# A four-layer graph network on one core: in the third layer, a copy and a read moved by one turn, and a row stored in two parts

## The chip, the core and the metric

The kernel runs on one core of a Trainium2 chip. A core has five engines that run their own instruction streams and wait for each other by semaphores: TensorE (PE, its weight loads PEld), VectorE (DVE), ScalarE (ACT), GpSimd (POOL) and SyncE (SP, which here only issues DMAs). GpSimd issues the gathers (indirect DMAs), SyncE all other transfers. The metric is the device time of one execution in microseconds.

## What is computed

The reference takes 6250 nodes with 256 features and 100000 edges and applies four graph layers; after each, the layer's output is added to its input and normalised. The third layer, which the change is in, is two graph attention passes, one after the other:

```python
def _gat_layer(h_in, W, a_s, a_d, b, src, dst, n):
    h = (h_in @ W).reshape(n, Hh, Cc)                 # 4 heads of 64
    alpha_s = jnp.sum(h * a_s, axis=-1)
    alpha_d = jnp.sum(h * a_d, axis=-1)
    e = leaky_relu(alpha_s[src] + alpha_d[dst], 0.2)  # a self loop for each node is in src, dst
    ex = jnp.exp(e - segment_max(e, dst)[dst])
    alpha = ex / segment_sum(ex, dst)[dst]
    return segment_sum(h[src] * alpha[:, :, None], dst).reshape(n, Hh * Cc) + b
h = gelu(_gat_layer(x, W0, ...)); h = gelu(_gat_layer(h, W1, ...))
x = _layernorm(x + h)
```

The fourth layer needs, for each target, the sum of `x` over its edges. The kernel gets part of that as a dense product with a matrix of edge counts, and it makes this matrix beside the third layer.

## The kernel before

Nodes are cut into 50 blocks of 125 targets. Each block's edges, sorted by target, are 16 chunks of 128 edges; the few that don't fit are shared by 25 blocks. A pass of the third layer handles a block in four pieces of four chunks, so 200 pieces a pass. Each piece goes through steps in a fixed distance:

- `piece2` gathers its edges' rows of the table `hs` (features, source score, target score) by four indirect DMAs on GpSimd into one of ten buffers `g` (L929).
- `steps_of` adds the target's score to the source's (`e`, L2152), applies the leaky slope (`r`, L2154), takes exponentials on ScalarE (L2156, L2157), and multiplies the rows by them (L2160, VectorE).
- `one_hots` (L938, VectorE) makes the matrix that sends each edge to its target, and TensorE adds the rows up by target into a bank `ps` (L2227; L2220 adds the self loop). There are two such banks, so the block after next needs a bank back.
- `finish2` reads the finished sums (L2044 to L2046), and for each pair of blocks adds the bias, applies Gelu and multiplies by the next weights (first pass), or normalises and prepares the tables of the fourth layer (second pass).

`keys2` gets the targets' scores to the edges, a block ahead. SyncE loads the block's keys into `kb` (two buffers); ScalarE turns them into masks, in two halves of two pairs of instructions (`node_hots`, L947 and L948); TensorE multiplies them with the scores in 48 small products into a bank `pe`, 24 for each half (L2185); ScalarE copies the bank to `ends_d` (L2190, three buffers). There is one bank `pe`: the products of the next block can't begin before this copy.

`count_edges` makes the count matrix, a step now and then beside the pieces. VectorE makes weighted one-hots (L1995), TensorE adds them up (L2005). Three ranges of 500 targets share a float32 word (one byte each), and a row block of 125 sources has two such words. For each word ScalarE copies the sum to an integer (L1981) and spreads its bytes out (L1982) into half of `a_row`, 3000 bytes a source with one buffer. After the second word the whole row block is stored to `a_table`. Every transfer of 125 rows through `move` (L807 to L811) is two DMAs, of 112 and 13 rows.

The order of TensorE's, VectorE's and ScalarE's work is written out by the class `Turns`. A piece, a block's keys or a finish is a generator that names, at each `yield`, the group of work that it goes on with. In each turn the groups are stepped in the order "e", "msg", "fin", "fa", "act", "pe", "ps", "late", "new", "keys". A plain name means the next turn; a number before it ("2act") means so many turns later; a "+" means in this turn, if the group's place has not passed. A turn takes one new piece in, so a block is four turns. `run_pass` adds a block's keys eight turns ahead of its first piece. Turns only set the order on each engine: an engine that is ready runs on into later turns, and another can be turns behind.

So the copy L2190 of a block stands in the second turn after its last small product, and the finish reads a block's sums in the third turn after its last sum.

Of the kernel before, what the change touches and what calls it, by code (L numbers as in the profile page):

```python
# [9 lines left out]
U8 = mybir.dt.uint8  # L10
# [646 lines left out]
def gnn_stack_kernel(ctx: ExitStack, tc: tile.TileContext, ins, out):  # L657
# [13 lines left out]
    nc = tc.nc  # L671
# [4 lines left out]
    B = max(p for p in range(1, P + 1) if N % p == 0)  # L676
# [36 lines left out]
    ND, RB, WORD = 24, 4, 3  # L713
    RW, NR = RB * B, ND // RB
# [28 lines left out]
    with ExitStack() as fast:  # L743
# [885 lines left out]
        with tc.tile_pool(name="f0", bufs=1) as pool, tc.tile_pool(name="f0w", bufs=2) as work, tc.tile_pool(  # L1629
            name="f0v", bufs=1  # L1630
# [316 lines left out]
        def count_edges():  # L1947


            column = ap.tile([P, RW], F16, name="a_column", bufs=1)  # L1950
            nc.vector.scalar_tensor_tensor(
                column.rearrange("p (b n) -> p b n", n=B), iota[:, :RB, None].to_broadcast([P, RB, B]), float(B),
                iota_p[:, None, :B].to_broadcast([P, RB, B]), op0=ALU.mult, op1=ALU.add,
            )
            end, over = (
                ap.tile([P, 3, RW], BF16, name="a_hot", bufs=4).rearrange("p i j -> p (i j)").bitcast(F32)[:, : NB * DC]
                .rearrange("p (b c) -> p b c", c=DC) for _ in range(2)
            )
            nc.vector.tensor_copy(end, idx_s[:, :, :DC])
            unit = [ap.tile([P, NB, DC], F32, name=f"a_unit{w}", bufs=1) for w in range(NW)]  # L1960
            nc.vector.memset(unit[0], 1.0)
            for w in range(1, NW):
                nc.vector.memset(unit[w], 0.0)
            less = ap.tile([P, NB, DC], F32, name="a_less", bufs=1)
            nc.vector.tensor_copy(less, end)
            for r in range(1, NR + 1):
                nc.vector.tensor_single_scalar(over, end, float(r * RW), op=ALU.is_ge)
                nc.vector.scalar_tensor_tensor(less, over, -float(RW), less, op0=ALU.mult, op1=ALU.add)
                for w, by in ((r // WORD, 256.0 ** (r % WORD)), ((r - 1) // WORD, -(256.0 ** ((r - 1) % WORD)))):
                    if w < NW:  # L1970
                        nc.vector.scalar_tensor_tensor(unit[w], over, by, unit[w], op0=ALU.mult, op1=ALU.add)
            yield
            steps = [(s, *slot) for s in range(NB) for slot in slots]
            sts, rows, accs, hots, done = {}, {}, {}, {}, []
            for k in range(len(steps) + 4):
                if done and done[0][2] <= k:
                    s, w, _ = done.pop(0)
                    if w == 0:
                        rows[s] = ap.tile([B, ND * B], U8, name="a_row", bufs=1)
                    word = ap.tile([B, RW], I32, name="a_word", bufs=1)  # L1980
                    nc.scalar.copy(word, accs.pop((s, w))[:B])  # L1981
                    nc.scalar.activation(  # L1982
                        rows[s][:, w * WORD * RW : (w + 1) * WORD * RW].rearrange("p (q j) -> p q j", q=WORD),
                        word.bitcast(U8).rearrange("p (j q) -> p q j", q=4)[:, :WORD, :], AF.Copy,
                        accum_out=counted[:B, s * NW + w : s * NW + w + 1],
                    )
                    if w == NW - 1:
                        move(nc.sync, a_table[s * B : (s + 1) * B, :], rows.pop(s))
                if k < len(steps):
                    s, w, c0, n, _, _ = steps[k]  # L1990
                    if s not in sts:
                        sts[s] = one_hots(ap, key_s[:, s, :DC], DC, DC, 2, BF16, "a_st")
                    hots[k] = ap.tile([P, 3, RW], BF16, name="a_hot", bufs=4)
                    for i in reversed(range(n)):
                        nc.vector.tensor_scalar(  # L1995
                            hots[k][:, i, :], column, less[:, s, c0 + i : c0 + i + 1],
                            unit[w][:, s, c0 + i : c0 + i + 1], op0=ALU.is_equal, op1=ALU.mult,
                        )
                if 0 <= k - 1 < len(steps):
                    s, w, c0, n, first, last = steps[k - 1]  # L2000
                    hot = hots.pop(k - 1)
                    if first:
                        accs[s, w] = apsum.tile([P, 512], F32, name="a_acc", bufs=2)[:, :RW]
                    for i in range(n):
                        nc.tensor.matmul(  # L2005
                            accs[s, w], sts[s][:, c0 + i, :], hot[:, i, :], start=(first and i == 0),
                            stop=(last and i == n - 1),
                        )
                    if last:
                        done.append((s, w, k + 2))  # L2010
                        if w == NW - 1:
                            del sts[s]
                yield
# [15 lines left out]
        for layer in range(2):  # L2029
# [142 lines left out]
            def keys2(b):  # L2172
                kb = work.tile([B, CAP], BF16, name="kb")
                move(nc.sync, kb, keys_d[b : b + 1, :].to_broadcast([B, CAP]))
                yield "2keys"
                ts = kb.rearrange("p (c e) -> p c e", e=P)
                for half in range(2):
                    node_hots(kb, 2 * half)
                    node_hots(kb, 2 * half + 1)
                    yield "pe"  # L2180
                    if half == 0:
                        pe = psum.tile([P, CM, H2], F32, name="pe")
                    for c in range(CM // 2 * half, CM // 2 * (half + 1)):
                        for k in range(3):
                            nc.tensor.matmul(  # L2185
                                pe[:, c, :], ts[:, c, :], ad_parts[:, b, k, :], start=(k == 0), stop=(k == 2)
                            )
                    yield "2act" if half else "+keys"
                ends_d[b] = work.tile([P, CM, H2], F32, name="ends_d", bufs=3)
                nc.scalar.copy(ends_d[b], pe)  # L2190

            def piece2(b, c0, n):
                if c0 == 0:
                    if b % GB == 0:
                        turns.add(shared2(b // GB))
                    held[b] = work.tile([B, 1, D + 8], F32, name="own", bufs=4)
                    move(nc.sync, held[b][:, 0, :], block_rows(table, b))
                g = gp.tile([P, 4, D + 8], F32, name="g")
                for i in reversed(range(n)):
                    gather(g[:, i, :], table[:, :], idx_d[:, b, c0 + i : c0 + i + 1])  # L2200
                yield "2e"
                steps = steps_of(g, n, ends_d[b][:, c0 : c0 + n, :], (c0 // 4) % 2)
                next(steps)
                if c0 == 0:
                    own = held[b]
                    mine = steps_of(own, 1, own[:, :, D + 4 :], 3, B)
                    next(mine)
                yield "msg"
                for _ in steps:
                    pass  # L2210
                if c0 == 0:
                    for _ in mine:
                        pass
                st = one_hots(work, key_d[:, b, c0 : c0 + n], n, 4, ST_BUFS)
                if c0 + n == CM:
                    st_s = one_hots(work, key_d[:, b, CM:], SH, SH, 3, name="st_s")
                yield "ps"
                if c0 == 0:
                    sums[b] = psum.tile([P, 512], F32, name="ps", bufs=2)
                    nc.tensor.matmul(  # L2220
                        sums[b][:B, : D + H2], ident[:B, :B], held[b][:, 0, : D + H2], start=True, stop=False
                    )
                from_all = [(c0 + i, st[:, i, :], g, i) for i in range(n)]
                if c0 + n == CM:
                    from_all = [(-1, st_s[:, h, :], shared[b // GB], h) for h in range(SH)] + from_all
                for c, hot, m, i in from_all:
                    nc.tensor.matmul(  # L2227
                        sums[b][:B, : D + H2], hot, m[:, i, : D + H2], start=False, stop=(c == CM - 1)
                    )
                if c0 + n == CM:  # L2230
                    del held[b], ends_d[b]
                    yield "3fin"
                    yield from finish2(b, layer)

            made = pieces((4, 4, 4, 4))
# [247 lines left out]
```

## Time and profile before

| | us |
|---|---|
| median of 3 runs (lowest, highest) | 5936.43 (5924.23, 5954.35) |
| the profiled execution | 5892.39 |
| its span | 5890.5 |
| start of the third layer's first pass, 2695 to 2775 | 80 |
| its steady part, 2775 to 3895 | 1120 |
| end and start of the second pass, 3895 to 4000 | 105 |
| its steady part, 4000 to 5127 | 1127 |
| end of the third layer, 5127 to 5180 | 53 |
| fourth layer, 5180 to 5890 | 710 |

Over the span TensorE is busy 70%, VectorE 62%, ScalarE 50% and GpSimd 61%, and the mean granted clock of TensorE is 0.836 of full speed. The profiled execution is 44 us faster than the median of the other runs, so a sum made on its rows is carried to the median as a ratio.

In the lines of the profile, a group of instructions has its source line, engine, operation, output and inputs, then "| busy us, mean ns of one | idle us of the engine before them" and what ended that idle time. In lists of waits, "A <- B: us, times, longest" says that A was idle until B. "issue" is idle time that nothing in the profile ended, and "remote" is a release whose source isn't known. A releaser is inferred from the semaphores; where it had long been done, it was another.

### The profile page before, as it was taken

The numbers are of one execution on the slowest core, as the hardware profiler recorded it, in microseconds if no ns is written. First come the engines' busy times: TensorE is split into PE (matmuls) and PEld (weight loads), VectorE is DVE, ScalarE is ACT, GpSimd is POOL, SyncE is SP. The second block draws the span as 40 slices with busy tenths as digits, with TensorE's granted clock in tenths as the row PEclk, the third lists the DMA queues.
The fourth block names the chain that finished last, engine by engine and source line by source line (L and its number), as shares of the span: only waits on it lengthen the run. The fifth ranks groups of instructions, "written<-read, shape, count | busy, mean of one in ns | idle before, by whom it ended". The sixth has DMA issues, their size and how long they took to land. (4 is left out here: it accounts for less than half of the span.)

```text
span 5890.5 us, 79635 instructions
## 1 busy us (share of the span) xinstructions
PE 4107.0 (70%) x25027; PEld 3010.6 (51%) x25027; DVE 3632.0 (62%) x9526; ACT 2948.2 (50%) x7453; POOL 3595.0 (61%) x3710
## 2 busy tenths in 40 slices
PE   0567788875777777773666766656776677769996
PEld 0355666663555566552554554544555555535554
DVE  7786666653767777773656656645766667613454
ACT  4015676882666676662454445533555555422331
POOL 5776666654666666653666666646666666556663
PEclk9788899997888888886777788777878878889998
DMA  6555565554666777763444444434545455477883
GB/s 157 141 165 159 157 158 155 153 149 143 204 204 206 208 211 210 207 189 86 132 135 134 135 137 136 133 101 123 146 139 140 138 147 140 118 197 221 235 238 102
DMA packets 409642, 940.75 MB, mean 160 GB/s; under 512 B 96973, under 2 KB 214331, under 8 KB 409211
## 3 DMA queue, kind: packets, MB, share of 16 engines
q0 software_dynamic: 221184, 670.83, 41.3%
q1 hardware_dynamic: 188026, 264.74, 15.3%
q8 instruction: 201, 3.29, 0.2%
q14 instruction: 231, 1.88, 0.1%
HBM read 848.02 MB, written 87.21 MB: 159 GB/s over the span
## 5 line engine op out<-in xcount | busy, mean ns | idle before, releaser
L929 POOL DMA_INDIRECT g<-hs_table_f,idx_d x1600 | 1527.6, 955 | 920.5 <-issue 453.1
L929 POOL DMA_INDIRECT g<-h_table_f,idx_d x800 | 802.0, 1002 | 435.2 <-issue 212.3
L2227 PE MATMUL ps<-g,st 128*125 128x260 f32 x3200 | 955.0, 445 | 116.6 <-issue 108.9
L929 POOL DMA_INDIRECT g<-kv_table_f,idx_s x784 | 744.8, 950 | 448.8 <-issue 289.4
L2160 DVE TENSOR_TENSOR g<-g,iota_p 128x1024 f32<-128x1024 f32 x400 | 488.4, 1221 | 654.6 <-ACT iota_p L2156 312.4
L2227 PEld LDWEIGHTS ps<-g,st 128*125 128x125 f32 x3200 | 712.7, 224 | 320.9 <-issue 151.0
L2185 PE MATMUL pe<-ad_parts,kb 125*128 125x4 bf16 x4800 | 220.1, 165 | 631.7 <-issue 543.1
L963 PE MATMUL ps<-g,st 128*128 128x256 bf16 (+1 forms) x3648 | 525.2, 300 | 136.3 <-issue 61.3
L929 POOL DMA_INDIRECT g<-x_table_f,idx_d x416 | 397.8, 956 | 289.3 <-issue 158.8
L963 PEld LDWEIGHTS <-st 128*128 128x128 bf16 x4104 | 427.8, 106 | 283.1 <-issue 130.3
L2185 PEld LDWEIGHTS <-kb 125*128 125x128 bf16 x4800 | 185.0, 99 | 721.8 <-issue 603.4
L1920 PE MATMUL ps<-g,st 128*125 128x264 f32 x1600 | 470.2, 442 | 28.1 <-issue 20.2
L947 ACT ACTIVATE kb<-kb,minus 125x512 bf16<-125x512 bf16 x600 | 426.2, 711 | 58.3 <-DMA g<-kv_table_f,idx 20.4
L948 ACT ACTIVATE kb<-kb,ones 125x512 bf16<-125x512 bf16 x600 | 432.6, 721 | 20.6 <-ACT kb L947 1.5
L2393 PE MATMUL d<-cnt,xs 125*128 125x500 bf16 x1800 | 403.7, 378 | 36.5 <-issue 20.4
L938 DVE TENSOR_TENSOR st<-iota_p,key_d 128x500 f32<-128x500 f32 (+1 forms) x550 | 410.6, 747 | 0.0
L1920 PEld LDWEIGHTS ps<-g,st 128*125 128x125 f32 x1600 | 344.9, 220 | 112.3 <-issue 28.9
L1903 DVE TENSOR_TENSOR prod<-g,qe 128x1024 f32<-128x1024 f32 x200 | 243.2, 1216 | 246.5 <-PE ps L1920 96.7
L2156 ACT ACTIVATE iota_p<-r 128x16 f32<-128x16 f32 (+2 forms) x504 | 90.9, 180 | 591.0 <-DVE e L2152 217.6
L1889 PE MATMUL qe<-q,kb 125*128 125x256 bf16 x2400 | 324.0, 288 | 65.6 <-issue 32.5
L1515 ACT ACTIVATE ob<-t_f,s_f 125x128 bf16<-125x128 f16 x800 | 310.3, 388 | 96.1 <-remote 65.1
L1889 PEld LDWEIGHTS <-kb 125*128 125x128 bf16 x2400 | 247.8, 103 | 141.6 <-issue 77.6
(458 smaller groups left out, 8051.4 us busy)
## 6 DMA issues: line engine op xcount, KB each, us to landing
kb<-keys_d_f SPq DMA_DIRECT2D x100, 448.0 KB
g<-hs_table_f,idx_d POOLq DMA_INDIRECT x1600
xs<-x_table_f SPq DMA_DIRECT2D x75, 336.0 KB
kb<-keys_s_f SPq DMA_DIRECT2D x50, 448.0 KB
a_table_f<-a_row SPq DMA_DIRECT2D x50, 328.1 KB
few<-a_table_f SPq DMA_DIRECT2D x75, 218.8 KB
g<-h_table_f,idx_d POOLq DMA_INDIRECT x800
g<-kv_table_f,idx_s POOLq DMA_INDIRECT x784
```

What stands on the lines that cost most here:

```text
L929: nc.gpsimd.indirect_dma_start(out=g, out_offset=None, in_=table, in_offset=bass.IndirectOffsetOnAxis(ap=idx, axis=0))
L938: nc.vector.tensor_tensor(st, iota_p[:, None, :w].to_broadcast([P, n, w]), key[:, :, None].to_broadcast([P, n, w]), op=ALU.is_equal,)
L947: nc.scalar.activation(part, part, AF.Square, bias=minus[:B])
L948: return nc.scalar.activation(part, part, AF.Relu, bias=ones[:B, 0:1], scale=-1.0)
L963: nc.tensor.matmul(ps[:, :m], st[:, i, :], g[:, i, k * D : k * D + m], start=(c0 + i == 0 and k == 2), stop=(c0 + i == CH - 1 and k == 0),)
L1515: nc.scalar.activation(ob[:, i, :], o1[:, i, :], AF.Copy, scale=val_b[:, at])
L1889: nc.tensor.matmul(qe[:, i, :], ts[:, c0 + i, :], q[:, k * D : (k + 1) * D], start=(k == 0), stop=(k == 2))
L1920: nc.tensor.matmul(sums[b][:B, : D + H1], hot, m[:, i, D - H1 :], start=(c == 0), stop=(c == CM - 1))
L2160: nc.vector.tensor_mul(feats, feats, pp[:, :, :, None].to_broadcast([p, n, H2, C2]))
L2185: nc.tensor.matmul(pe[:, c, :], ts[:, c, :], ad_parts[:, b, k, :], start=(k == 0), stop=(k == 2))
L2227: nc.tensor.matmul(sums[b][:B, : D + H2], hot, m[:, i, : D + H2], start=False, stop=(c == CM - 1))
L2393: nc.tensor.matmul(accs[h][q], xs[:, i, j * D + h * P : j * D + (h + 1) * P], cnt[:, i, q * RW : (q + 1) * RW], start=(s + i == 0 and j == 2),
```

## The change

Three edits, all in the third layer's passes.

1. In `keys2`, the copy of the targets' scores to `ends_d` comes three turns after the block's last small product in place of two.
2. In `piece2`, `finish2` begins four turns after the block's last sum in place of three.
3. In `count_edges`, each word of a row block has a buffer of its own of 1500 bytes a source, of which there are two, and is stored right after it is made; before, both words stood in one buffer of 3000 bytes and were stored together.

```diff
@@ count_edges @@
-            sts, rows, accs, hots, done = {}, {}, {}, {}, []
+            sts, accs, hots, done = {}, {}, {}, []
             for k in range(len(steps) + 4):
                 if done and done[0][2] <= k:
                     s, w, _ = done.pop(0)
-                    if w == 0:
-                        rows[s] = ap.tile([B, ND * B], U8, name="a_row", bufs=1)
+                    row = ap.tile([B, WORD * RW], U8, name="a_row", bufs=NW)
                     word = ap.tile([B, RW], I32, name="a_word", bufs=1)
                     nc.scalar.copy(word, accs.pop((s, w))[:B])
                     nc.scalar.activation(
-                        rows[s][:, w * WORD * RW : (w + 1) * WORD * RW].rearrange("p (q j) -> p q j", q=WORD),
+                        row.rearrange("p (q j) -> p q j", q=WORD),
                         word.bitcast(U8).rearrange("p (j q) -> p q j", q=4)[:, :WORD, :], AF.Copy,
                         accum_out=counted[:B, s * NW + w : s * NW + w + 1],
                     )
-                    if w == NW - 1:
-                        move(nc.sync, a_table[s * B : (s + 1) * B, :], rows.pop(s))
+                    move(nc.sync, a_table[s * B : (s + 1) * B, w * WORD * RW : (w + 1) * WORD * RW], row)
@@ keys2 @@
-                    yield "2act" if half else "+keys"
+                    yield "3act" if half else "+keys"
                 ends_d[b] = work.tile([P, CM, H2], F32, name="ends_d", bufs=3)
                 nc.scalar.copy(ends_d[b], pe)
@@ piece2 @@
                 if c0 + n == CM:
                     del held[b], ends_d[b]
-                    yield "3fin"
+                    yield "4fin"
                     yield from finish2(b, layer)
```

## The prediction

> **What bounds the kernel now.** I read the page's busy shares, the stretches of the span by stage, the waits of each engine inside the two attention passes of the third layer, and the timelines of one block. The change touches only these two passes (2775 to 3895 us, and 4000 to 5127 us), so only their limits matter.
>
> The page says that no engine is full over the span. The last line shown here is the row to remember: the small products `pe` keep TensorE idle for 631.7 us, of which 543.1 us ended with no releaser ("issue").
>
> ```profile
> PE 4107.0 (70%) x25027; PEld 3010.6 (51%) x25027; DVE 3632.0 (62%) x9526; ACT 2948.2 (50%) x7453; POOL 3595.0 (61%) x3710
> L929 POOL DMA_INDIRECT g<-hs_table_f,idx_d x1600 | 1527.6, 955 | 920.5 <-issue 453.1
> L2185 PE MATMUL pe<-ad_parts,kb 125*128 125x4 bf16 x4800 | 220.1, 165 | 631.7 <-issue 543.1
> ```
>
> The stretches (length, then busy time and count of PE, PEld, DVE, ACT, POOL, then the granted clock, the DMA share and GB/s) show the same picture in both passes: 1120 and 1127 us for about 47.5 blocks each, so some 23.6 us a block.
>
> ```profile
> 2775.00:3895.00 1120.00, 759.45 (x4749) 568.18 (x4749) 675.05 (x1624) 541.45 (x1219) 724.63 (x762) 0.79 0.48 133
> 4000.00:5127.00 1127.00, 797.60 (x4866) 583.42 (x4865) 757.81 (x1973) 570.92 (x1316) 730.68 (x763) 0.80 0.50 139
> ```
>
> Next, who waits for whom between 2800 and 3880 us (total us, times, longest), first on TensorE, then on ScalarE:
>
> ```profile
> PE pe L2185 <- issue: 263.5, 242, 2.7
> PE ps L2227 <- issue: 38.2, 41, 2.2
> PE pe L2185 <- ACT kb L947: 8.2, 2, 7.3
> PE pe L2185 <- remote: 4.3, 1, 4.3
> ```
>
> ```profile
> ACT ends_d L2190 <- PE ps L2220: 86.2, 17, 9.3
> ACT ends_d L2190 <- PE ps L2227: 66.9, 15, 10.5
> ACT a_row L1982 <- DMA a_table_f<-a_row: 36.5, 7, 12.8
> ```
>
> TensorE is busy 68% of the first pass, and its idle time is nearly all "issue": 263.5 + 38.2 + 12.8 + 8.2 + 1.3 = 324 us in these 1080 us. Waits for another engine or a DMA come to 19 us there, and to 12 us in 4000 to 5120 us. So TensorE has work that is ready all the time. ScalarE's waits for `pe` are long because TensorE is late, not the other way round.
>
> The timelines of TensorE and of GpSimd around 3310 us show what "issue" is:
>
> ```profile
> 3307.54 0.16 PE L2185 MATMUL pe<-ad_parts,kb 125*128 125x4 bf16 x1 [0.54 <-issue]
> 3309.68 0.17 PE L2185 MATMUL pe<-ad_parts,kb 125*128 125x4 bf16 x1 [1.25 <-issue]
> 3312.54 0.78 PE L2220 MATMUL ps<-own,ident 125*125 125x260 f32 x1 [1.25 <-issue]
> 3314.34 3.10 PE L2227 MATMUL ps<-g,st 128*125 128x260 f32 x8
> ```
>
> ```profile
> 3311.34 0.95 POOL L929 DMA_INDIRECT g<-hs_table_f,idx_d  x1 [0.30 <-issue]
> 3314.33 0.95 POOL L929 DMA_INDIRECT g<-hs_table_f,idx_d  x1 [2.04 <-DVE rdens L2044]
> ```
>
> Once a block, during the second half of `pe`, TensorE gets on at one instruction per 0.7 us for some 8 us. That ends about 1.5 us after GpSimd pauses (here at 3312.29), and GpSimd pauses because all ten gather buffers wait for TensorE's sums. The two take turns: 16 gathers at 1.25 us are 20 us, and pauses of 2 to 2.8 and about 1.2 us make 23.6. GpSimd's waits for anything but "issue" in 2800 to 3880 us are some 190 us. This alternation bounds the passes; vector and scalar engines follow it. Why TensorE slows the trace doesn't say.
>
> **The change, part by part.**
>
> *Copy of the targets' scores a turn later* (L2190, 100 copies of 0.21 us). It removes nothing and adds nothing; it moves each copy behind one more piece's two exponentials (0.17 + 0.20 us) and behind the masks L947/L948 of the next block's first half. ScalarE's waits at this copy (189.5 + 149.1 + 82.6 + 45.1 + 9.9 = 476 us over both passes) shrink, but they are slack: credit 0. Its price is the single `pe` bank: the next block's `pe` can't begin before the copy. I lined up, for all 99 pairs, the end of the exponentials behind which the copy will stand with the start of the next block's `pe`. The slack has a median of 4.1 us; it is negative in 21 cases, with 49 us together. That is an upper estimate, as these times still contain the waits that go away: taking each copy's own wait off leaves 13 negative cases with 31 us, of which 19 us lie at pass starts and ends, where TensorE has other cover or waits for gathers. I take +8 us, ends 0 and +49. What hides the rest is the wait of 4 to 5 us that ScalarE no longer has a turn earlier; without it every pair would lose about 3 us.
>
> A rule speaks against this part: the Trainium skill (PSUM — Partial Sum Buffer, Summary: rules for kernel authors) says to evacuate promptly. Were TensorE waiting for the bank, a delay of one turn's ScalarE work (3.2 us from copy to the new place, from the timeline: two mask pairs and two exponentials) in 100 blocks would cost 320 us. But the row "who waited for `ends_d`" has TensorE with 7.4 us, once, in the whole run. I take the row.
>
> At the start of the first pass the new order gains: the copy waits until 2760.26 us, and the two mask pairs that stood behind it (2760.37 to 2763.1) now run before it, in that wait. First exponentials come 2.7 us earlier: −2.7 us. In the second pass the first piece waits for its gather (9.5 us), so nothing.
>
> *Block sums read four turns behind* (L2044 to L2046: 0.15 + 0.18 + 0.42 us, 100 blocks). Same work. VectorE waits there 103.7 us for "remote" and 32 us more by name; these move or vanish, and VectorE isn't the bound: 0. Everything of the block's ending follows a turn later (bias and Gelu with two table loads of 1.28 us, transposes, weights' product, the store of `hs`), and as the copy moves too, their order against it stays. The two banks `ps` must be free when the block after next begins: lining up L2220 with the end of the next turn's VectorE work, the least slack is 4.3 us and the median 14.8, so no wait: 0. The price without that cover would be VectorE's turn, about 5 us a block. In the last turns of a pass nothing stands between the two turns, so the tables of the next layer are ready as before: 0, at most one turn's VectorE work (3 us) a pass.
>
> *Each word of a row stored by itself.* ScalarE's copies stay (100 of 0.56, 1.45 and 0.19 us). One row buffer of 3000 B becomes two of 1500 B, so ScalarE no longer waits for the store before (50.6 us, 13 times): off the bounding pair, 0, with up to −10 us where this made ScalarE late for `pe` (2800 to 3880 us has 8.2 + 1.8 us of TensorE waiting for masks). Each store is two DMAs, so 100 more on SP's queue, at 309 and 389 ns: 35 us of SP, which spends some 900 us of each pass (435.6 + 353.5 + 138.3 in the first) waiting for TensorE to free `kb` and `own`. Bytes stay (18.75 MB); packets grow by 6,250 of 409,642 if a row of a store is one. The new first-word store stands in SP's queue before a `kb` or `own` load, but waits for a ScalarE instruction that runs earlier than TensorE's release of `kb`, for which the load waits anyway: 0, at worst 1 us in some blocks (+25).
>
> Here a rule speaks against the change too: the Trainium skill (DMA: Bandwidth & Descriptors, Anatomy of one DMA) puts some 2.0 us of fixed time on each DMA, stated for the gpsimd path. In series 100 more would be an estimate of +200 us; by the row they stand on a queue that waits, and nobody waits for a store but the row buffer that is now doubled. I take the row.
>
> **Sum** on the profiled execution's 5892.4 us (span 5890.5): −2.7 + 8 − 5 (half of the mask waits) + 0 = 0. The median of the runs shown is 5936.4, 44 us above this execution; a forecast against the median is 5936 us, ratio 1.000.
>
> **The rivals.**
>
> *It gets slower: the `pe` bank becomes the wait.* Place: first `pe` product of each block, behind the copy, behind one more turn of exponentials, which wait for VectorE. It decides once ScalarE's lead over TensorE falls under one turn (5.9 us) in most blocks; then each pays 1 to 3 us and GpSimd's pause grows by as much: +100 to +250 us, 6035 to 6190. For it: one bank, 21 negative slacks. Against: median 4.1 us, and ScalarE gains lead.
>
> *It gets faster: scalar and vector engines run a turn further ahead, and TensorE never waits.* All its named waits in the passes (31 us) go, and GpSimd's pauses shrink by up to as much again: −30 to −60 us, 5876 to 5906. For it: some 660 us of waits (476 + 136 + 51) are taken up by name. Against: none sits on TensorE or GpSimd.
>
> *The turn-taking shifts.* The slow stretches fall on other instructions, since the streams are placed anew. A slow stretch stopped TensorE for 28 us at 3970 to 3998; one more or less of these, or 0.4 us a block, is ±40 us: 5896 or 5976. Nothing in the profile gives the sign.
>
> *The changed waits are hidden anyway*: my forecast.
>
> **How the numbers follow.** Hidden: 0.50, with 5936 and a range of its own from 5910 to 5963. Slower by the bank: 0.16. Faster by the lead: 0.14. Shifted turns: 0.20, half each way, of which about 0.04 on each side stay within 0.5%, which is about what a measurement of this kernel can tell from no change (30 us; the three runs span as much). Of the hidden case 0.05 falls beyond on the slow side (the +25 and +49 ends) and 0.02 on the fast side. So slower 0.16 + 0.06 + 0.05 = 0.27, faster 0.14 + 0.06 + 0.02 = 0.22, same 0.51. The range, 5880 to 6010, reaches to both ends of the shifted turns and past the +49 and +25 together; it leaves out the bank's case (0.16) and the far end of the lead (0.04).
>
> **What would show it.** Right: the passes stay within 10 us of 1120 and 1127; waits at the copy fall from 476 us to under 300; the wait of `a_row` for its store falls under 10 us; that of `rdens` under 40 us; "issue" before `pe` stays at 240 to 290 us a pass. Wrong, towards slower: a row of TensorE's `pe` waiting for ScalarE's `ends_d` with over 100 us. Wrong, towards faster: "issue" before `pe` or GpSimd's pauses shrink by over 50 us, so that those waits had held the alternation after all. Wrong for the stores: SP waiting for `a_row` longer than for TensorE, and masks L947 waiting for `kb`.

## The result, and the profile after

| | before | changed |
|---|---|---|
| median of 11 runs each, one chip (lowest, highest), us | 5939.87 (5924.23, 5954.35) | 5977.55 (5955.75, 5987.93) |
| ratio, 95% interval | | 1.0055 (1.0044 to 1.0067) |
| the profiled execution, us | 5892.39 | 5973.72 |
| first gather of the third layer, us | 2695.7 | 2723.9 |
| first pass, first to last gather, us | 1198.4 | 1207.1 |
| second pass, first to last gather, us | 1189.2 | 1231.5 |
| last of these gathers to the end, us | 764.1 | 767.7 |

The changed kernel is slower by 0.55%, some 33 us by this ratio (38 us by the medians). The two profiled executions differ by more, by 81 us: the one of before lies below all of its other runs, and 28 us of the difference lie ahead of the third layer, in code that is the same. What is left of it is in the two passes, and most of that in the second: +42 us, against +9 in the first.

The stretches of the span in the changed kernel (length, busy time and count of PE, PEld, DVE, ACT, POOL, granted clock, DMA share, GB/s):

```profile
2803.00:3932.00 1129.00, 748.66 (x4747) 563.97 (x4745) 672.94 (x1622) 544.07 (x1218) 723.82 (x761) 0.79 0.47 132
4037.00:5205.00 1168.00, 793.23 (x4877) 587.80 (x4876) 752.52 (x1959) 566.10 (x1306) 729.47 (x763) 0.79 0.48 134
```

The steady part of the second pass went from 1127 to 1168 us, while TensorE's busy time there did not grow (797.60 before, 793.23 now) and the clock is the same within 0.01. So the 41 us are idle time on TensorE, not slower work.

Some of the waits in the second pass of the kernel before, on TensorE (4000 to 5120 us), ScalarE (3990 to 5110 us) and GpSimd (4027 to 5042 us):

```profile
PE pe L2185 <- issue: 240.2, 216, 7.4
PE ps L2227 <- issue: 59.3, 77, 2.0
ACT y L2120 <- remote: 37.1, 10, 7.0
POOL g L929 <- PE ps L2227: 43.2, 27, 3.2
POOL g L929 <- remote: 18.3, 9, 2.9
```

And in the changed kernel's second pass from 4037 to 5197 us, on TensorE, then on ScalarE, then (4064 to 5118 us) on GpSimd:

```profile
PE pe L2183 <- issue: 253.3, 224, 2.7
PE ps L2225 <- issue: 76.6, 74, 2.3
PE a_acc L2003 <- issue: 15.7, 14, 2.2
```

```profile
ACT y L2118 <- remote: 66.0, 10, 11.2
ACT ends_d L2188 <- PE pe L2183: 60.3, 9, 15.1
ACT a_word L1980 <- remote: 44.7, 8, 7.0
ACT ends_d L2188 <- PE ps L2225: 35.5, 7, 8.8
ACT y L2118 <- PE ps L2225: 22.9, 4, 11.7
```

```profile
POOL g L929 <- PE ps L2225: 90.3, 33, 8.8
POOL g L929 <- remote: 59.2, 24, 3.1
```

TensorE's waits for other engines and DMAs stay small (23 us here by name, the longest 6.4 us), and none of them is of `pe` for `ends_d`, so the bank `pe` is not the cause. ScalarE's waits moved, as was meant, from the copy `ends_d` to others, among them the copy of `y` out of `fin`. On GpSimd there are new pauses of 4 to 9 us: in the kernel before, the second pass has two of over 4 us behind its start, and here ten.

One of them, at 4356 us, on TensorE, ScalarE and GpSimd of the changed kernel:

```profile
4341.40 3.67 PE L2225 MATMUL ps<-g,st 128*125 128x260 f32 x16
4344.90 1.03 PE L2106 MATMUL fin<-w_lr,aT 128*125 128x256 f32 x4
...
4347.52 1.05 PE L2111 MATMUL fin<-aT,w_lr 128*128 128x125 f32 x8
4348.41 0.80 PE L2003 MATMUL a_acc<-a_hot,a_st 128*128 128x500 bf16 x3
4349.04 0.59 PE L2183 MATMUL pe<-ad_parts,kb 125*128 125x4 bf16 x18
...
4357.11 0.18 PE L2183 MATMUL pe<-ad_parts,kb 125*128 125x4 bf16 x1 [0.55 <-issue]
4358.52 1.89 PE L2225 MATMUL ps<-gs,st_s 128*125 128x260 f32 x4 [1.23 <-issue]
4360.21 2.67 PE L2225 MATMUL ps<-g,st 128*125 128x260 f32 x8
```

```profile
4348.65 0.37 ACT L2118 COPY y<-fin 125x256 f32<-125x256 f32 x1 [4.35 <-PE fin L2111]
4358.59 0.37 ACT L2118 COPY y<-fin 125x256 f32<-125x256 f32 x1 [9.57 <-remote]
```

```profile
4355.23 0.95 POOL L929 DMA_INDIRECT g<-hs_table_f,idx_d  x1 [0.30 <-issue]
4363.15 0.94 POOL L929 DMA_INDIRECT g<-hs_table_f,idx_d  x1 [6.97 <-PE ps L2225]
```

And the same place in the kernel before (TensorE, then GpSimd):

```profile
4286.24 1.92 PE L2227 MATMUL ps<-g,st 128*125 128x260 f32 x8
4287.99 1.03 PE L2108 MATMUL fin<-w_lr,aT 128*125 128x256 f32 x4
...
4290.61 1.05 PE L2113 MATMUL fin<-aT,w_lr 128*128 128x125 f32 x8
4291.50 1.92 PE L2227 MATMUL ps<-g,st 128*125 128x260 f32 x8
4293.26 0.80 PE L2005 MATMUL a_acc<-a_hot,a_st 128*128 128x500 bf16 x3
4293.89 0.69 PE L2185 MATMUL pe<-ad_parts,kb 125*128 125x4 bf16 x22
```

```profile
4307.51 0.94 POOL L929 DMA_INDIRECT g<-hs_table_f,idx_d  x1 [3.17 <-PE ps L2227]
```

What the reader is to see is the place of the 3.7 us of `fin` products (L2108 and L2113, now L2106 and L2111: the fourth layer's weights, once per pair of blocks). Before, they stood between the second and the third piece of a block. Now they stand behind the third, straight ahead of a half of `pe` and of the block's last piece, which has twelve sums in place of eight. The copy of `y` reads them and now waits through TensorE's slow stretch.

These rows allow two readings, and I took the wrong one first: that ScalarE's wait at `y` holds up the exponentials behind it, and with them TensorE and GpSimd. The other is that the place of the product on TensorE counts, whoever reads it.

### The profile page after: what moved, and what is told of

It is laid out like the page before. It is cut to its first block, busy times and chain, and to the rows that moved or that the text cites. A ratio compares the mean times of both kernels' runs of the same rounds, so it can differ in the third digit from the quotient of the medians.

```text
span 5971.8 us, 79722 instructions
## 1 busy us (share of the span) xinstructions
PE 4093.0 (69%) x25027; PEld 3004.4 (50%) x25027; DVE 3630.9 (61%) x9526; ACT 2949.7 (49%) x7453; POOL 3582.2 (60%) x3710
## 5 line engine op out<-in xcount | busy, mean ns | idle before, releaser
L2225 PE MATMUL ps<-g,st 128*125 128x260 f32 x3200 | 938.6, 442 | 95.4 <-issue 88.5
```

The costliest lines, as they stand in the source:

```text
L2225: nc.tensor.matmul(sums[b][:B, : D + H2], hot, m[:, i, : D + H2], start=False, stop=(c == CM - 1))
```

## The experiments

All runs are timed against the kernel before on the same chip. This matters here. The five groups of runs met very different times of the kernel before: 5892.23 and 5883.49 us in two, 5068.28, 5068.72 and 5066.59 us in three, beside 5939.87 us above. In the three groups near 5068 us TensorE's slow stretches are missing from the traces, and with them what was to be tested; several kernels were therefore run twice.

### Each part alone

The kernel before with one of the edits, and with the first two together (`e1_copy`, `e2_finish`, `e3_store`, `e4_copy_finish`):

```diff
# e1_copy, and in e4_copy_finish
-                    yield "2act" if half else "+keys"
+                    yield "3act" if half else "+keys"
# e2_finish, and in e4_copy_finish
-                    yield "3fin"
+                    yield "4fin"
# e3_store: the edit of count_edges as in the change
```

> The kernel before with the copy of the targets' scores a turn later, and nothing else. Finish theory (the later end of a block is what costs): ratio 0.998 to 1.002, second pass within 10 us of 1127, waits at the copy fall from 476 us over both passes to under 300 without a gain. Copy theory (ScalarE's wait for the slow stretch of pe moves from the copy to the next instruction that needs TensorE, with the exponentials behind it): 1.004 to 1.007, second pass about 1160, GpSimd's pauses of 7 to 9 us in it. Store theory: 1.000. Combination theory (copy and finish only cost together): 0.998 to 1.002.

> The kernel before with the end of a block four turns behind its last sum in place of three, and nothing else. Finish theory: 1.004 to 1.007, of it 30 to 40 us in the second pass, where the copy of y out of fin waits for TensorE with some 60 us more than before and GpSimd pauses for 7 to 9 us about every 100 us; first pass within 12 us. Copy theory and store theory: 0.998 to 1.002. Combination theory: 0.998 to 1.002, since the copy of the targets' scores still takes ScalarE's wait a turn earlier.

> The kernel before with each word of a row of counts in its own buffer and stored by itself, and nothing else. Store theory (100 more DMAs on SP's queue make the loads of kb and own late, or the place of the conversion's wait changes): 1.004 to 1.007, with waits for kb or own on ScalarE or TensorE of over 30 us. All others: 0.998 to 1.001; the wait of a_row for its store (50.6 us before) is gone in any case.

> The kernel before with the copy a turn later and the end of a block a turn later, stores as before. Combination theory: 1.004 to 1.007 although each alone is at 1.000. Finish theory: as the finish alone, 1.004 to 1.007. Copy theory: as the copy alone, 1.004 to 1.007. Store theory: 0.998 to 1.001, second pass within 10 us of 1127.

| beside 5892.23 us | ratio | second pass, us |
|---|---|---|
| copy alone | 0.9999 (0.9987 to 1.0010) | 1191.5 |
| finish alone | 1.0024 (1.0013 to 1.0035) | 1205.1 |
| stores alone | 0.9997 (0.9985 to 1.0010) | 1191.9 |
| copy and finish | 1.0039 (1.0025 to 1.0053) | 1218.0 |

The copy and the stores cost nothing by themselves; every kernel with the later finish is slower, and in the second pass. That rules out the copy and the store theory as I had put them, and the combination theory too, since the finish alone costs. Its ratio is less than the finish theory expected, and its interval overlaps with that of copy and finish: whether the copy adds something on top of the finish isn't settled.

### Product, reader or front

The finish is a chain of steps: the sums and the normalisation, the transposes, the copies `aT`, the product in `fin`, the copy of `y`. Four kernels take the chain apart. One changed kernel reads `y` a turn later; one has the product (and all that follows it, the copies of `y` and `xr` and their stores) back where it stood, with all that is ahead of it still a turn later; one is the kernel before with the product and what follows it a turn later, and nothing else; one keeps the later finish for the first pass only.

```diff
# e5_read and f5_read: the changed kernel, second pass
-                    yield "3act"
+                    yield "4act"
                     y = work.tile([B, 2, D], F32, name="y", bufs=1)
# e6_product_back and f6_product_back: the changed kernel, second pass
-                    yield "3act"
+                    yield "2act"
                     xTs = [kept(work, pt, "aT") for pt in pts]
# e7_product_late and f7_product_late: the kernel before, second pass
-                    yield "late"
+                    yield "2late"
                     dense = b < ND
# e8_first_only: the changed kernel
-                    yield "4fin"
+                    yield "4fin" if layer == 0 else "3fin"
```

> The changed kernel with the copy of y out of fin (second pass) four turns behind its product in place of three; nothing else. Reading theory: the fourth layer's product in fin now stands right ahead of the half of pe in which TensorE is slow, its end reaches ScalarE only when the slow stretch is over, and the exponentials that stand behind the copy of y come late. Then a later copy gives the second pass back: 1231 us falls to 1190 to 1210, ratio to before 0.999 to 1.003, the waits at y of over 5 us fall from 8 to 3 or fewer, GpSimd's pauses of over 4 us in the pass from 11 to 5 or fewer. Front theory (the sums, the normalisation and the transposes a turn later are what costs): 1.004 to 1.007 as before this edit. Place theory (24 more matmuls in the turn of that half are what costs, whoever reads them): 1.004 to 1.007.

> The changed kernel with the copies aT of the second pass two turns behind the transposes in place of three, so that the product in fin and the copy of y stand again where they stood before the change; sums, normalisation and transposes stay a turn later. Reading theory and place theory: second pass 1190 to 1205, ratio 0.999 to 1.002, GpSimd's pauses of over 4 us 5 or fewer. Front theory: second pass 1220 or more, 1.004 to 1.007.

> The kernel before with one edit: in the second pass the product in fin, and with it the copy of y, a turn later; the start of a block's end, the copy of the targets' scores and the stores as before. Reading theory and place theory: second pass 1200 to 1225 in place of 1189, ratio 1.001 to 1.004, GpSimd's pauses of over 4 us 7 or more. Front theory: 1189 plus or minus 5, ratio 0.999 to 1.001.

> The changed kernel with the later end of a block in the first pass only; in the second it is three turns behind, as before. All theories that put the cost into the second pass's end of a block: second pass 1185 to 1200, ratio 0.998 to 1.001. If the copy and the stores cost by themselves when both are made: second pass 1205 or more, ratio 1.002 or more.

Beside a kernel before of 5068.28 us they gave 0.9997 (0.9989 to 1.0006), 0.9993 (0.9985 to 1.0002), 1.0005 (0.9997 to 1.0013) and 0.9996 (0.9988 to 1.0004). The waits of the last one in 3400 to 4360 us, its second pass, on GpSimd and on TensorE say why nothing can be told apart here:

```profile
POOL g L929 <- issue: 176.2, 578, 0.3
POOL g L929 <- PE ps L2225: 15.5, 51, 0.3
```

```profile
PE pe L2183 <- ACT ends_d L2188: 120.8, 43, 7.0
PE fin L912 <- DVE x_sb L2091: 43.5, 22, 5.3
PE ps L2225 <- DVE st L938: 42.7, 27, 4.2
PE ps L2225 <- issue: 5.4, 2, 4.4
```

GpSimd never waits for more than 0.3 us: 16 gathers of 1.25 us are 20 us a block, and 50 blocks are 1000 us of the pass's 1019. The 240 to 290 us a pass of "issue" ahead of `pe` on TensorE are gone. So three of these kernels were run again, with the changed kernel beside them:

> The changed kernel as it is, beside the kernel before. Two cases, told apart by the kernel before. Where it takes about 5900 us, TensorE has its slow stretches: ratio 1.004 to 1.007, GpSimd's pauses of over 4 us in the second pass 8 or more. Where it takes about 5070 us, as beside the four runs before this one, there are none: 0.999 to 1.001, since nothing is left that a reader of a product could wait for. If the cost doesn't come from the slow stretches, it is 1.004 to 1.007 in both.

> The changed kernel with the copy of y four turns behind its product, once more. Where the kernel before takes about 5900 us: reading theory 0.999 to 1.003, second pass 1190 to 1210; front theory and place theory 1.004 to 1.007. Where it takes about 5070 us: 0.999 to 1.001 for all.

> The changed kernel with the product in fin and the copy of y back at their old turn, the front of a block's end still a turn later, once more. Where the kernel before takes about 5900 us: reading theory and place theory 0.999 to 1.002, second pass 1190 to 1205; front theory 1.004 to 1.007. Where it takes about 5070 us: 0.999 to 1.001 for all.

> The kernel before with the product in fin and the copy of y a turn later in the second pass, and nothing else, once more. Where the kernel before takes about 5900 us: reading theory and place theory 1.001 to 1.004, second pass 1200 to 1225; front theory 0.999 to 1.001. Where it takes about 5070 us: 0.999 to 1.001 for all.

| beside 5883.49 us | ratio | second pass, us |
|---|---|---|
| changed | 1.0043 (1.0026 to 1.0059) | 1209.0 |
| changed, `y` read a turn later | 1.0027 (1.0011 to 1.0043) | 1213.2 |
| changed, product and `y` back | 1.0002 (0.9989 to 1.0015) | 1192.2 |
| before, product and `y` late | 1.0054 (1.0034 to 1.0073) | 1200.6 |

The product's place carries the loss: moved by itself it costs as much as the change (1.0054, more than I had expected; the profiled execution is the fastest of its six), moved back it costs nothing, though sums, normalisation and transposes are still late. This rules out the front theory. What follows the product moved with it in both kernels; none moves the product without its followers.

It also rules out the reading theory, my first, as what makes the loss. In the kernel before with the product late, ScalarE hardly waits for `y` in the second pass (4003 to 5128 us), and the loss is there:

```profile
ACT y L2120 <- remote: 3.5, 5, 1.8
```

In the kernel with the product back, ScalarE waits for `y` as it does in the changed kernel beside it (97.4 us), and pays nothing. Its waits at that copy, 4000 to 5115 us, sum to 102.8 us:

```profile
ACT y L2118 <- remote: 48.1, 11, 10.5
...
ACT y L2118 <- PE ps L2225: 35.8, 15, 7.1
...
ACT y L2118 <- PE fin L925: 10.6, 4, 5.7
...
ACT y L2118 <- PE a_acc L2003: 8.3, 2, 5.3
```

And in the kernel with `y` read later these waits are gone (5.0 us in the whole pass), but eight of GpSimd's pauses of over 4 us behind the pass's start stay (ten in the changed kernel beside it, two with the product back), and the second pass stays long (its waits in 3995 to 5130 us):

```profile
POOL g L929 <- PE ps L2225: 77.5, 33, 8.9
POOL g L929 <- remote: 59.5, 28, 3.0
```

Its ratio, 1.0027, lies in the range that I had set for the reading theory, and below the 1.0043 of the changed kernel; the two intervals overlap. Whether the wait for `y` adds a part to the loss isn't settled.

What goes with the place can be read from the ends of the pieces' sums on TensorE. I took, for each piece of the second pass (blocks 4 to 45), the time from the last sum of the piece before to its own last sum. A gather buffer comes free at these ends, and with ten buffers the end of piece 3 of a pair (the last of its first block) frees the buffer of piece 13, which is the second of a later pair's second block. The table has the means, in us:

| kernel | interval to the end of piece 2 | to the end of piece 3 (longest) | GpSimd's idle time in the gathers of piece 13 | of all eight pieces |
|---|---|---|---|---|
| before | 5.8 | 8.3 (13.8) | 2.6 | 16.8 |
| copy alone | 5.7 | 8.5 (13.2) | 2.7 | 16.9 |
| stores alone | 5.8 | 6.3 (11.4) | 3.0 | 16.9 |
| changed, product back | 5.8 | 7.4 (12.2) | 2.3 | 16.8 |
| finish alone | 2.2 | 14.6 (19.8) | 3.8 | 17.2 |
| before, product late | 2.2 | 12.4 (19.9) | 4.0 | 17.4 |
| changed, `y` later | 2.2 | 11.6 (19.6) | 4.4 | 17.7 |
| copy and finish | 2.2 | 13.3 (20.7) | 4.7 | 18.0 |
| changed, second group | 2.2 | 13.0 (19.5) | 4.4 | 17.7 |
| changed | 2.2 | 12.4 (19.7) | 5.2 | 18.8 |

The table splits the kernels in two. Where the product has moved, the interval to piece 2 is 3.6 us shorter than in the kernel before and the one to piece 3 is 3 to 6 us longer, with up to 21 us in which nothing is freed. GpSimd's idle time grows at piece 13, which waits for piece 3's buffer; in five of the six kernels it falls at piece 12, by 0.5 to 0.9 us. (In every piece 1.2 us of idle are four gathers' own 0.3 us.) Over 25 pairs a pass, the last column gives 10 to 50 us, where the passes are 11 to 42 us longer than before's.

This shows where GpSimd stands still, and not yet why. The shift alone doesn't put off the end of piece 3: the two intervals sum to 14.1 us in the kernel before, to 12.1 to 14.2 us in the other kernels without the loss, and to 13.8 to 16.8 us in those with it. By the gaps between TensorE's records, the interval to piece 3 is 5.7 us of work and 2.6 us of idle time in the kernel before, and 8.8 and 3.6 us in the changed kernel: the product, and a longer stretch. Nor is length alone what counts: the interval to a pair's first piece, where the largest part of TensorE's idle time falls, has a mean of 11.0 to 13.7 us in all ten kernels, with the loss or without.

In the first pass the same shift puts a product of 1.7 us from the interval to piece 1 (4.5 us before) into that to piece 2 (2.2 before, 3.9 after), both short, and the pass shows no loss: 1195.6 to 1207.1 us in the kernels with the later finish, 1195.9 to 1202.5 in those without.

### Where else the product could stand, and one more buffer

Two things were left: whether any long interval would do, and whether a longer lead of GpSimd takes the pause away. The kernel before with the product two and three turns later in the second pass, and both kernels with eleven gather buffers:

```diff
# h1_two / h2_three and j_three: the kernel before, second pass
-                    yield "late"
+                    yield "3late"          # h2_three, j_three: "4late"
                     dense = b < ND
# g11_changed and j_g11_changed: the changed kernel; g11_before: the kernel before
-        G_BUFS, ST_BUFS = 10, 6
+        G_BUFS, ST_BUFS = 11, 6
-... name="a_hot", bufs=4)
+... name="a_hot", bufs=3)
```

> The kernel before with the product in fin and the copy of y two turns later in the second pass, and nothing else: the product then stands behind the last piece of a block and ahead of the second half of pe. Release theory (what counts is the longest interval in which TensorE frees no gather buffer): the product's 3.7 us are in the interval that holds the second half of pe and often the slow stretch, so it costs again, 1.001 to 1.006, with GpSimd's longer pause a piece later, before the third piece of an odd block. Pile theory (the product costs only where it stands straight ahead of the first half of pe and the last piece's twelve sums, the longest piece): 0.999 to 1.001. Where the kernel before takes about 5070 us and has no slow stretches: 0.999 to 1.001 by both.

> The kernel before with the product in fin and the copy of y three turns later in the second pass: the product stands between the first and the second piece of a block, in an interval of 2.3 us. Release theory and pile theory: 0.998 to 1.001, second pass 1184 to 1196, no more than 4 pauses of over 4 us. A theory of mere lateness (the later a block's end, the dearer): 1.006 or more. Where the kernel before takes about 5070 us: 0.999 to 1.001.

> The changed kernel with eleven gather buffers in place of ten (and three a_hot buffers in place of four, to make room). Release theory: piece 3 of a pair then frees the buffer of piece 14 in place of 13, GpSimd has 5 us more of lead, and the pause behind the product goes: 1.000 or less against the kernel before, and as near to the next kernel as the two kernels are at the pass's other pauses (within 0.2%). If the slow stretch lasts until GpSimd pauses, whatever the lead, the pause stays and the ratio is 1.003 to 1.007. Where the kernel before takes about 5070 us: 0.999 to 1.001.

> The kernel before with eleven gather buffers (and three a_hot buffers). If the lead sets the pauses: GpSimd's pauses over 1 us, 268 and 236 us a pass before, shrink by a third or more and the time falls to 0.96 to 0.99. If the slow stretch lasts until GpSimd pauses: the stretches get longer by what the lead gives, 0.998 to 1.002. Where the kernel before takes about 5070 us: 0.999 to 1.001.

> The changed kernel with eleven gather buffers and three a_hot buffers, once more. Where the kernel before takes about 5900 us: release theory 1.000 or less against it, and GpSimd's extra pause before the second piece of an odd block (4.4 to 5.2 us a pair with ten buffers, 2.3 to 3.0 in the kernels without the loss) falls under 3; if the slow stretch lasts until GpSimd pauses, whatever the lead, 1.003 to 1.007, the pause standing one piece later. Where it takes about 5070 us: 0.999 to 1.001.

> The kernel before with the product in fin and the copy of y three turns later in the second pass, once more. Where the kernel before takes about 5900 us: release theory and pile theory 0.998 to 1.001, second pass 1184 to 1196; mere lateness 1.006 or more. Where it takes about 5070 us: 1.000 to 1.002, as beside the runs before this one.

Both groups met kernels before of 5068.72 and 5066.59 us, without slow stretches. Two turns later: 1.0000 (0.9991 to 1.0008). Three turns later: 1.0015 (1.0008 to 1.0022) and 1.0012 (1.0003 to 1.0021). Eleven buffers: 0.9998 (0.9989 to 1.0006) and 1.0002 (0.9993 to 1.0012) changed, 0.9997 (0.9988 to 1.0005) before. Without slow stretches GpSimd makes no pause that a buffer could take away, so the question of the lead stays open, and so does that of other places. They show one thing. With the changed kernel and eleven buffers the longest mean interval without a freed buffer is 14.5 to 14.7 us in the second pass, as long as in the slow kernels above, and GpSimd doesn't pause. So a long interval doesn't cost by its length. That it costs where GpSimd has no buffers in hand, as where TensorE keeps falling behind, is my reading; no run here tests it. The small loss three turns later, 6 to 8 us, I can't place: the profiled second passes are 1029.9 and 1023.1 us, against 1019 to 1027 for the others of that kind.

No version was faster than the kernel before. The changed kernel with the product put back is level with it.

## Why the prediction was wrong

The time, 5977.55 us, lies in the range (5880 to 6010), but the forecast was no change, and the kernel lost 0.55% (0.44 to 0.67). That it lies in the range is in part luck: the +49 and the +25 that were to fit below its upper end didn't come.

**The step that failed** is the cost of the block sums read four turns behind, and in it this sentence: "Everything of the block's ending follows a turn later (bias and Gelu with two table loads of 1.28 us, transposes, weights' product, the store of `hs`), and as the copy moves too, their order against it stays." I had costed it at 0 by three covers: VectorE isn't the bound, the `ps` banks have slack, and the order against the copy stays. All three are covers for other steps. What moved as well is the second pass's product, on TensorE itself, one of the two engines that I had named as the bound; and its order against the pieces' sums doesn't stay. The trace of before had both numbers: 3.7 us of product from 4287.99, followed by another piece's sums, and a last piece with twelve of them. The term should have been 3.7 us of TensorE's work that passes one release of gather buffers in each of 25 pairs: from 0, if the work only changes places, to 25 × 3.7 = 92 us as an upper estimate. In its place the runs showed 1.0054, some 32 us, with the product and its followers moved by themselves, and 1.0002 with them put back; the six second passes with the product late are 11 to 42 us longer.

**The bound** was right where there are slow stretches: TensorE's stretches and GpSimd's gathers in alternation. I took the stretches for part of the kernel; three groups of runs show kernels of the same code around it without them, and there the product a turn later is at 1.0005 (0.9997 to 1.0013). "Once a block" I had read from the first pass, where the long intervals are those to each block's first piece (12.7 and 12.5 us). In the second pass of the kernel before, 7.4 of TensorE's 13.7 us of idle time a pair fall ahead of the pair's first piece, so the two blocks of a pair are not alike, and it was the second pass that lost.

**The copy a turn later**: forecast +8, with ends of 0 and +49. Alone it is at 0.9999, −0.6 us by the ratio (interval −7.7 to +5.9). Going against the rule of prompt evacuation cost nothing that can be measured here. In the changed kernel the waits at the copy fell from 476 us to 305 over both passes (124.8 + 79.6 + 50.8 + 49.6), just short of the sign of "under 300", and without a gain. The sign that I had set for the bank as the wait, over 100 us of `pe` waiting for `ends_d`, does appear in runs without slow stretches, with 120.8 us in the kernel whose second pass has the copy late and the finish early; and there the ratio is 0.9996, since GpSimd's gathers are the bound. In no trace with slow stretches that I read does it appear.

**The stores by word**: forecast −5, with ends of −10 and +25. Alone they are at 0.9997, −1.8 us (−8.8 to +5.9). The wait of `a_row` for its store is gone, and in that kernel no wait for `kb` or `own` took its place; the fixed time of a DMA that I set against this row stays hidden, as the row had it.

**The signs.** The first pass is within 10 us of 1120 (1129), the second isn't (1168 against 1127). The waits at `rdens` fell from 136 to 97 us over both passes, not to under 40. "Issue" ahead of `pe` is 287.4 and 253.3 us, in the band that I had set for "no change" (240 to 290), though the kernel is slower: the sign was too coarse, as a loss of 41 us is spread over several rows of TensorE.

**The rivals.** The bank (6035 to 6190) and the gain from ScalarE's lead didn't come. "The turn-taking shifts", with 0.4 us a block or 5976 us, has the size and the kind: the streams placed anew against the slow stretches. But I had written that nothing in the profile gives the sign. Whether the place of the product in TensorE's timeline could have given it beforehand, the runs don't say; it is where to look.

**What stays open.** Why TensorE has slow stretches, why some chips or runs have none, and by what way the product's place makes the loss. In the rows above the stretch itself fell ahead of the last piece, and TensorE's idle time in that interval is 2.8 to 4.9 us a pair in the kernels with the product late, against 2.6 in the kernel before; but whether the product's place draws the stretch there, the runs can't tell. Nor can they tell the product's own part from that of what follows it. Whether another buffer would take the pause away wasn't seen. Nor is it settled why the loss differs between the kernels with the late product, from 1.0024 to 1.0055.

## What to carry to other kernels

When a step is moved by a turn, follow every instruction that it issues to its new neighbours on the engine that bounds the stage; whether its order against the other moved step stays says nothing about that. Where an engine works in bursts and another lives on the buffers that it frees, ask which release the moved work will now stand ahead of, and not only for the sum of the work: 3.7 us a pair, moved past one release, went with up to 42 us in a pass of 1190 with no work added. And a long wait on a third engine, right beside the loss, is not its cause until a kernel without the wait has been timed.

## What the runs showed of the hardware

The kernel before took between 5883 and 5940 us in three groups of runs (medians) and between 5067 and 5069 in three others, a seventh less, and there all runs of this kernel in a group are within 0.3%. The difference runs through the whole kernel: with the later finish in the first pass only, the third layer's first gather starts at 2316.4 us, against 2695.7 us in the kernel before of the slower kind. In the second pass TensorE's granted clock is 0.85 in place of 0.80, but its busy time shrinks only from some 798 us to 750. What goes is the idle time without a releaser: "issue" ahead of `pe`, 240.2 us in 3990 to 5110 us of the kernel before, falls to nothing, and GpSimd's pauses with it. The product and what follows it a turn later gave 1.0054 in one group with stretches and 1.0005 in one without. The changed kernel itself wasn't run without them; with eleven buffers it was, at 0.9998 and 1.0002. What decides between the two kinds of groups the runs don't show.

In one place that the rows show, a product that ran just ahead of a slow stretch reached its reader only when the stretch was over. The second product in `fin` ends at 4348.57 us in the records of TensorE; ScalarE, idle and waiting for it, started at 4358.59 us, 0.07 us after TensorE's first sum behind the stretch (the profile has the release as "remote"). Ends on TensorE are modelled, so the product may have ended later than the row says; for the reader, the start of the first sums behind the stretch was the better clue here.
